# An output projection in seven half-size products per pair of token tiles, with every engine in program order up to a check

## The chip, the cores and the metric

The kernel runs on one core of a Trainium2 chip. The core has a matrix engine (TensorE, PE in the profile), a vector engine (VectorE, DVE), an activation engine (ScalarE, ACT), a general engine (GpSimd, POOL) and an engine that mostly issues transfers (SyncE, SP). Matrix products are written to PSUM[...]; the other data sit in SBUF, and large arrays in device memory, from and to which DMA transfers move them. The metric is the device time of one execution in microseconds (us); lower is better.

## The reference

An image of 48 by 48 tokens with 768 channels goes through a transformer block and then through a spectral layer. What matters here is the joint between attention and MLP:

```python
attn = softmax(q @ k^T * scale + rel_h + rel_w)      # 12 heads of 64
out  = attn @ v                                       # 2304 tokens x 768
out  = out @ proj_w + proj_b                          # <- the part that is changed
x    = shortcut + out
xn2  = layernorm(x)
h    = gelu(xn2 @ mlp_w1 + mlp_b1)
x    = x + (h @ mlp_w2 + mlp_b2)
# then the spectral layer: rfft2, two block-diagonal complex layers, irfft2, + x
```

All of it is in 32-bit floats. The output projection is a product of 2304 x 768 with 768 x 768.

## The kernel before, in words

The 2304 tokens are 18 tiles of 128 (`NT`), the 768 channels 6 blocks of 128 (`NC`); `CH` and `G` are 384[...]. The kernel runs in stages: queries, keys and values; attention for six pairs of heads, six chunks of 384 queries each; the output projection; the MLP in three passes of 768 tokens; the spectral layer.

**How the order is set.** A planner orders the instructions of each engine ahead of time by its own cost estimates. Inside a `tc.manual_schedule` region the engines it names keep the order in which the program writes them; where such a region's instructions fall among those of the same engine outside it remains the planner's. In attention PE, SP, ACT and DVE are in program order and POOL is the planner's. In the first half of the projection only PE is in program order. In the second half everything is the planner's.

**The end of attention.** For the last chunk, `left_apart` (L641) stores the inverse denominators, `spread_out` (L654) loads them back spread over the partitions, `scaled` multiplies (DVE, L666) and adds the value bias (POOL, L669), and `stored` (L675) writes the chunk to `oT` in device memory. Both transfers and the store are issued on SP.

**The projection.** `outputs(t)` (L754) loads one token tile `og` of `oT`, channels first. `residual(t)` loads a tile of the input into `x1` (L747) and adds the bias on POOL (L748). `projected(psum, t, og)` makes both 384-wide halves of the tile: six matmuls each into one bank (L761), then one DVE add of the bank into `x1` (L765). The weights `pw` are loaded during attention. `x1` lies in the buffer that holds the exponentials during attention, so a tile of `x1` can be loaded once the last chunk's products have read that part.

**The check and the two halves.** Attention skips the usual subtraction of the row maximum. The sums and the inverses of the denominators are therefore checked (L781 to L794), and a general path under `tc.If` (L801) recomputes attention where they are out of bounds; it is not taken with this data. Tiles 0 to 8 are projected before the check, tiles 9 to 17 after it. All engines meet at the check. In the second half the layer norm of tiles 0 to 5 (`normalise`, L121 to L129), their bias add (POOL, L995), the transposes to channels-first (`transposed`, L139 to L145) and the sums that the MLP's products need (`sums_of_tokens`, L177) are worked in between. The MLP's first weights and their sums on POOL (L159 to L168) are also moved up into it by the planner.

**Seven products instead of eight.** The queries, keys and values and the MLP already multiply blocked matrices by Strassen's scheme in Winograd's form: a 2 x 2 product of blocks takes seven block products and some sums of blocks instead of eight products. `left` and `right` make the sums of the two operands, and `queries_and_keys`, `values` and `hidden` (L1060) the products.

Of the kernel before, what the change touches and what calls it, by code (L numbers as in the profile page):

```python
# [22 lines left out]
NT = T // P  # L23
# [23 lines left out]
def block_then_afno(  # L47
# [69 lines left out]
    def normalise(pool, src, hat=None, made=None):  # L117

        stats = pool.tile([P, 2, 6], F32, name="stats")
        for i in range(2):  # L120
            nc.vector.bn_stats(stats[:, i, :], src[:, ts(i, C // 2)])  # L121
        mv = pool.tile([P, 2], F32, name="mv")
        nc.vector.bn_aggr(mv, stats.rearrange("p a b -> p (a b)"))
        rstd = pool.tile([P, 1], F32, name="rstd")
        nc.scalar.activation(rstd, mv[:, 1:2], AF.Sqrt, bias=eps)
        nc.vector.reciprocal(rstd, rstd)
        if hat is None:
            hat = pool.tile([P, C], F32, name="hat", bufs=4)
# [64 lines left out]
    with ExitStack() as flag_scope:  # L193
# [12 lines left out]
        with ExitStack() as att:  # L206
# [338 lines left out]
            with tc.manual_schedule(engines={mybir.EngineType.PE, mybir.EngineType.SP}):  # L545
# [123 lines left out]
                        nc.gpsimd.tensor_scalar(o, o, col(V_VB + pr), None, ALU.add)  # L669
                        results.append((pr, c, o))  # L670

                def stored():
                    while results:
                        pr, c, o = results.pop(0)
                        nc.sync.dma_start(out=oT[ts(pr, P), ts(c, G)], in_=o)  # L675

                def between(pr, c, acc):

# [28 lines left out]
                with tc.manual_schedule(  # L707
                    engines={mybir.EngineType.Activation, mybir.EngineType.DVE}
                ):
                    for pr in range(NC):  # L710
                        for c in range(T // G):
                            if c == 1 and pr < NC - 1:
                                fetch(pr + 1, kv[(pr + 1) % 2])
                            if c == 3 and pr < NC - 1:
                                fetch_values(pr + 1)
                            if c == 4 and pr == NC - 1:
                                nc.sync.dma_start(
                                    out=pw, in_=proj_w.rearrange("(c p) f -> p c f", p=P)
                                )
# [12 lines left out]
                            for i in range(6):  # L732
                                for what in work.get(i, ()):
                                    what()
                                products(op, heads[pr][2], range(3 * i, 3 * i + 3))
                            finish(pr, c, op)
                    scaled(0)
                    stored()

        ln2 = flag_scope.enter_context(tc.tile_pool(name="ln2", bufs=4))  # L740
        for i in range(4):
            ln2.tile([P, C], F32, name="hat")
        pj = flag_scope.enter_context(tc.tile_pool(name="proj", bufs=6))

        def residual(t):

            nc.sync.dma_start(out=x1[:, t, :], in_=x[ts(t, P), :])  # L747
            nc.gpsimd.tensor_tensor(x1[:, t, :], x1[:, t, :], pb, ALU.add)  # L748

        def outputs(t, og=None):  # L750

            if og is None:
                og = pj.tile([P, NC, P], F32, name="og")
            nc.sync.dma_start(out=og, in_=oT[:, ts(t, P)].rearrange("(c p) t -> p c t", p=P))  # L754
            return og

        def projected(psum, t, og):
            for k in range(2):
                pp = psum.tile([P, CH], F32, name="pp", tag="o")
                for c in range(NC):  # L760
                    nc.tensor.matmul(  # L761
                        pp, og[:, c, :], pw[:, c, ts(k, CH)], start=(c == 0), stop=(c == NC - 1)
                    )
                half = x1[:, t, ts(k, CH)]
                nc.vector.tensor_tensor(half, pp, half, ALU.add)  # L765

        EARLY = NT // 2
        with tc.tile_pool(name="ps_flag", bufs=1, space=PSUM) as psum, tc.tile_pool(  # L770
            name="ps_early", bufs=6, space=PSUM
        ) as psum_early, tc.manual_schedule(engines={mybir.EngineType.PE}):
            early = {t: outputs(t) for t in range(3)}
            pb = pj.tile([P, C], F32, name="pb", bufs=1)
            nc.sync.dma_start(out=pb, in_=proj_b[0, :].partition_broadcast(P))
            b2 = pj.tile([P, C], F32, name="b2_early", bufs=1)
            nc.sync.dma_start(out=b2, in_=mlp_b2[0, :].partition_broadcast(P))
            residual(0)
            projected(psum_early, 0, early[0])
# [7 lines left out]
            for t in range(1, EARLY):  # L787
                if t == 2:
                    line = psum.tile([1, P], F32, name="line")
                    nc.tensor.transpose(line, both, ident)  # L790
                    all_f = flag_pool.tile([1, 1], F32, name="all_f")
                    nc.vector.tensor_reduce(all_f, line, AX.X, ALU.min)
                    all_i = flag_pool.tile([1, 1], I32, name="all_i")
                    nc.vector.tensor_copy(all_i, all_f)  # L794
                residual(t)
                projected(psum_early, t, early[t] if t in early else outputs(t))
            for t in range(EARLY, NT):
                residual(t)
            later = {t: outputs(t) for t in range(EARLY, EARLY + 3)}
        safe = nc.values_load(all_i[0:1, 0:1], min_val=0, max_val=1)  # L800
        with tc.If(safe < 1):  # L801
            with ExitStack() as att:
# [27 lines left out]
                for pr in range(NC):  # L830
# [39 lines left out]
                    for sg in range(T // SG):  # L870
# [56 lines left out]
                        for j in range(2):  # L927
                            for qt in range(SG // P):
# [51 lines left out]
            with tc.tile_pool(name="g_ps_proj", bufs=2, space=PSUM) as psum:  # L980
                for t in range(NT):
                    residual(t)
                for t in range(EARLY):
                    projected(psum, t, outputs(t))
                for t, og in later.items():
                    outputs(t, og)

        with tc.tile_pool(name="ps_proj", bufs=2, space=PSUM) as psum:
            hats = []
            for t in range(EARLY, NT):  # L990
                projected(psum, t, later[t] if t in later else outputs(t))
                n = t - EARLY
                if n < 6:
                    hats.append(normalise(ln2, x1[:, n, :]))
                    nc.gpsimd.tensor_tensor(x1[:, n, :], x1[:, n, :], b2, ALU.add)  # L995
                if n in (2, 5):
                    transposed(psum, hats, xt, n // 3, V_LN2G, V_LN2B, tag="t")
                    hats = []
                if n == 5:
                    sums_of_tokens(xt, xs)  # L1000


    turn = ctx.enter_context(tc.tile_pool(name="turn", bufs=6))
# [585 lines left out]
```

## Time and profile before

| what | value |
|---|---|
| median of 3 runs | 2863.26 us (2861.73 to 2863.7) |
| the profiled execution | 2862.67 us, of which the span of the trace is 2860.6 us |
| PE busy | 2811.8 us, 98% of the span |
| DVE busy | 1695.7 us, 59% |
| ACT busy | 916.4 us, 32% |
| POOL busy | 625.5 us, 22% |
| first matmul of the projection | at 1429.92 us |
| last matmul of it before the check, first after it | ends near 1499.97, starts at 1503.69 us |
| first matmul of the MLP | at 1579.95 us |

Times of instructions are counted from the start of the span. One 32-bit matmul shows as two records, each with a weight load that runs beside it, so the 216 matmuls of the projection are 432 records. A busy PE is not a PE at its peak; the ends of matmuls are modelled.

### The profile page before, as it was taken

Reading aid. Unit: us, or ns where it says so; the run is one execution under the profiler, and the core shown is the slowest. Engines: PE = TensorE matmul, PEld = TensorE weight load, DVE = VectorE, ACT = ScalarE, POOL = GpSimd, SP = SyncE. Lnnn points to the kernel's source line nnn. Section 1 sums busy time; section 2 is a strip of 40 time slices with the busy share of each in tenths; the row PEclk is TensorE's granted clock in tenths of the full one; section 3 lists DMA queues with packets and bytes.
Section 4 is the critical chain, followed back from the end, with each engine's and each line's share of the span. In section 5 each row is a group of like instructions: output and inputs, shape, how many; then the busy total and the mean of one; then the engine's idle time right before and its main releaser. Section 6 shows DMA issues by size and latency. Waiting matters only on the chain. (4 is left out here: it accounts for less than half of the span.)

```text
span 2860.6 us, 41333 instructions
## 1 busy us (share of the span) xinstructions
PE 2811.8 (98%) x15877; PEld 1733.5 (61%) x15877; DVE 1695.7 (59%) x2488; ACT 916.4 (32%) x1466; POOL 625.5 (22%) x625
## 2 busy tenths in 40 slices
PE   8999999999999999999999999999999999999998
PEld 4555665656566666665555555555555555556887
DVE  5343226666666767676614666675666566666665
ACT  1011125757565666665400211021111211102332
POOL 2303010000000000000043332343232322222433
PEclk9999999999999999999999999999999999999999
DMA  4323285374663737455342121121121212113254
GB/s 154 129 97 111 97 164 108 64 131 76 94 134 57 132 65 128 93 80 99 107 133 78 50 67 55 56 86 59 54 67 55 89 55 66 45 62 113 61 160 141
DMA packets 223629, 262.80 MB, mean 92 GB/s; under 512 B 24668, under 2 KB 204092, under 8 KB 221888
## 3 DMA queue, kind: packets, MB, share of 16 engines
q1 hardware_dynamic: 220984, 258.22, 36.8%
q8 instruction: 129, 2.11, 0.3%
q10 hardware_dynamic: 2440, 1.84, 0.2%
q14 instruction: 76, 0.62, 0.1%
HBM read 143.96 MB, written 52.31 MB: 69 GB/s over the span
## 5 line engine op out<-in xcount | busy, mean ns | idle before, releaser
L581 ACT ACTIVATE main<-sp 128x768 f32<-128x768 f32 x648 | 516.4, 811 | 34.9 <-PE sp L571 19.9
L725 DVE TENSOR_TENSOR pairs<-pairs,main 128x1536 f32<-128x1536 f32 x252 | 443.1, 1758 | 27.1 <-DVE pairs L725 0.9
L571 PE MATMUL sp<-terms,select 64*128 64x384 f32 x1296 | 413.8, 631 | 0.0
L1122 DVE TENSOR_TENSOR main<-o,main 128x384 f32<-128x384 f32 x540 | 299.2, 557 | 39.4 <-PE o L1120 1.1
L1060 PE MATMUL h<-shared,w 128*128 128x384 f32 x864 | 296.6, 486 | 0.8 <-issue 0.8
L562 PE MATMUL sp<-shared 64*128 64x384 f32 x1296 | 266.9, 487 | 2.2 <-DVE o L462 2.2
L562 PE MATMUL sp<-qT,kT 64*128 64x384 f32 x1296 | 264.1, 484 | 0.0
L451 PE MATMUL m<-main 128*128 128x384 f32 x756 | 246.0, 487 | 3.3 <-DVE main L177 2.4
L1060 PEld LDWEIGHTS h<-shared,w 128*128 128x128 f32 x864 | 164.0, 190 | 116.2 <-issue 2.6
L1060 PE MATMUL h<-shared,w1s 128*128 128x384 f32 x648 | 226.6, 486 | 0.0
L627 POOL TENSOR_TENSOR inverse<-inverse,rden 24x32 f32<-24x32 f32 x36 | 15.1, 418 | 959.7 <-DVE sums L626 916.2
L594 PE MATMUL op<-main,shared 128*64 128x384 f32 x1296 | 217.4, 488 | 0.0
L1066 ACT ACTIVATE hT<-c,vec 128x384 f32<-128x384 f32 x108 | 66.3, 615 | 468.8 <-DVE c L1072 468.8
L594 PE MATMUL op<-main,v 128*64 128x384 f32 x1296 | 216.4, 488 | 0.0
L725 DVE TENSOR_TENSOR pairs<-main 128x1536 f32<-128x1536 f32 x36 | 63.3, 1759 | 250.6 <-ACT main L581 250.6
L451 PEld LDWEIGHTS m<-main 128*128 128x128 f32 x756 | 142.9, 190 | 103.8 <-issue 4.4
L1072 DVE TENSOR_TENSOR c<-h,u 128x384 f32<-128x384 f32 x108 | 60.2, 557 | 212.3 <-PE h L1060 212.3
L1120 PE MATMUL o<-w2s,hs 128*128 128x384 f32 x432 | 175.0, 487 | 4.0 <-DVE hs L160 4.0
L571 PEld LDWEIGHTS sp<-terms,select 64*128 64x128 f32 x1296 | 126.3, 187 | 83.5 <-issue 0.5
L1120 PE MATMUL o<-w,hT 128*128 128x384 f32 x432 | 175.0, 487 | 1.7 <-DVE acc L1126 0.8
L1060 PEld LDWEIGHTS h<-shared,w1s 128*128 128x128 f32 x648 | 123.2, 190 | 85.8
L159 POOL TENSOR_TENSOR w1s<-w 128x384 f32<-128x384 f32 x36 | 36.5, 1013 | 596.9 <-DMA w<-in_mlp_w_dram 396.9
(165 smaller groups left out, 3984.8 us busy)
## 6 DMA issues: line engine op xcount, KB each, us to landing
w<-in_mlp_w_dram SPq DMA_DIRECT2D x72, 768.0 KB
terms<-col_parts SPq DMA_DIRECT2D x432, 72.0 KB
terms<-row_hi SPq DMA_DIRECT2D x216, 72.0 KB
terms<-row_lo SPq DMA_DIRECT2D x216, 72.0 KB
main<-in_qkv_w_dram SPq DMA_DIRECT2D x36, 384.0 KB
z<-zt SPq DMA_DIRECT2D x48, 192.0 KB
x<-in_x_blocks_dram SPq DMA_DIRECT2D x18, 384.0 KB
k_d<-o SPq DMA_DIRECT2D x36, 192.0 KB
```

Of the source, the lines that this page charges most:

```text
L159: eng.tensor_tensor(s[0], a21, a22, ALU.add)
L451: nc.tensor.matmul(bank, a[:, c, :], b[:, c, :], start=(first and c == 0), stop=(c == 2), skip_group_check=not first,)
L562: nc.tensor.matmul(sp[:, j, :G], kT[at, ts(kt, P)], qT[at, ts(c, G)], start=first, stop=not first,)
L571: nc.tensor.matmul(sp[:, j, :G], select[at, a % 2], ready[pr, c][at, a // 2, b], start=first, stop=not first,)
L581: nc.scalar.activation(p, sp[:, :, :G], AF.Exp, scale=HD**-0.5)
L594: nc.tensor.matmul(op[ts(j, 64)], v[:, kt, ts(j, 64)], exps[:, kt, j, :], start=(kt == 0), stop=(kt == NT - 1),)
L725: nc.vector.tensor_tensor(pairs, so_far, exps[:, ds(kt - 1, 2)], ALU.add)
L1060: nc.tensor.matmul(bank[i], a[:, c, :], b[:, c, :], start=(start and c == 0), stop=(c == 2), skip_group_check=not start,)
L1066: nc.scalar.activation(h[:, i, ts(k, G)], src, AF.Gelu, bias=col(V_B1 + 2 * n + i))
L1072: nc.vector.tensor_tensor(t, src, other, ALU.add)
L1120: nc.tensor.matmul(bank[k], a, b, start=start, stop=True, skip_group_check=not start)
L1122: nc.vector.tensor_tensor(dst, bank[k], dst, ALU.add)
```

## The change

- The projection works on **pairs of token tiles**. `og` holds two tiles, and one transfer loads both.
- **The first pair is plain**: `plainly` makes four halves of six matmuls, each half in its own bank (m0 to m3), with a DVE add into `x1`.
- **Pairs 1 to 8** use seven half products: 3 channel blocks of `og` times a quarter of the weights, three matmuls for each of seven products (`projected`). The weight sums (`sum_of_weights`, four DVE operations of 128 x 1152) are made once; the fourth overwrites a quarter of `pw` after the first pair has read it. The sums of the outputs (`sums_of_outputs`, four DVE operations of 128 x 384) are made for each pair, one pair ahead.
- In each pair product 1 is copied to SBUF by ACT; DVE adds it to product 6 (`v`) and `v` to product 7 (`v7`); POOL adds `v`, `v` and `v7` into three of the four `x1` halves; DVE adds products 5, 2, 4 and 3 into `x1`. Products 2, 4 and 3 go to the banks of products 1, 7 and 5.
- **Four pairs** (eight tiles) come before the check and five (ten tiles) after it; before it was nine and nine.
- **Up to the check** PE, SP, DVE, ACT and POOL are all in program order; after it the planner orders all of them, as before.
- The **last store** of attention is issued on POOL instead of SP.
- In the second half the layer norms, the transposes and the sums for the MLP come after pairs instead of tiles.
- The general path reloads `pw`, projects plainly and makes the weight sums again; it is not taken.

```diff
-                def stored():
+                def stored(queue=nc.sync):
...
-                    stored()
+                    stored(nc.gpsimd)
...
-        pj = flag_scope.enter_context(tc.tile_pool(name="proj", bufs=6))
+        pj = flag_scope.enter_context(tc.tile_pool(name="proj", bufs=2))
+        pws = pj.tile([P, 3, 3, CH], F32, name="pws", bufs=1)
...
+        def weight_parts():
+            return [pw[:, ds(3 * j, 3), ts(k, CH)] for k in range(2) for j in range(2)]
+        def sum_of_weights(i):
+            a11, a12, a21, a22 = weight_parts()
+            s1, s2, s4 = (pws[:, i] for i in range(3))
+            dst, a, b, op = (
+                (s1, a21, a22, ALU.add), (s2, s1, a11, ALU.subtract),
+                (s4, a12, s2, ALU.subtract), (a21, a11, a21, ALU.subtract),
+            )[i]
+            nc.vector.tensor_tensor(dst, a, b, op)
+        def sums_of_outputs(pool, og):
+            b11, b21, b12, b22 = (og[:, ds(3 * i, 3), j] for j in range(2) for i in range(2))
+            sums = pool.tile([P, 3, 3, P], F32, name="ogs")
+            right(nc.vector, b11, b12, b21, b22, [sums[:, i] for i in range(3)])
+            return sums
...
+        def projected(psum, pool, u, og, sums):
...
+            pairs_of = {
+                1: (b11, a11), 2: (b21, a12), 3: (b22, s4), 4: (t4, a22),
+                5: (t1, s1), 6: (t2, s2), 7: (t3, s3),
+            }
+            bank = [psum.tile([P, G], F32, name=f"m{i}") for i in range(4)]
...
+            def first(j, k, src):
+                nc.gpsimd.tensor_tensor(half(j, k), half(j, k), src, ALU.add)
+            def into(j, k, src):
+                nc.vector.tensor_tensor(half(j, k), src, half(j, k), ALU.add)
+            m1 = pool.tile([P, G], F32, name="pm1")
+            nc.scalar.copy(m1, product(0, 1, True))
+            v = pool.tile([P, G], F32, name="pu")
+            nc.vector.tensor_tensor(v, product(1, 6, True), m1, ALU.add)
+            first(0, 1, v)
+            first(1, 0, v)
+            v7 = pool.tile([P, G], F32, name="pu7")
+            nc.vector.tensor_tensor(v7, product(2, 7, True), v, ALU.add)
+            first(1, 1, v7)
+            into(1, 1, product(3, 5, True))
+            into(0, 0, product(0, 2, False))
+            into(0, 1, product(2, 4, False))
+            into(1, 0, product(3, 3, False))
+        EARLY, PAIRS = 4, NT // 2
...
-        ) as psum_early, tc.manual_schedule(engines={mybir.EngineType.PE}):
-            early = {t: outputs(t) for t in range(3)}
+        ) as psum_early, tc.tile_pool(name="proj_early", bufs=2) as pe, tc.manual_schedule(
+            engines={
+                mybir.EngineType.PE, mybir.EngineType.SP, mybir.EngineType.DVE,
+                mybir.EngineType.Activation, mybir.EngineType.Pool,
+            }
+        ):
+            og = {0: outputs(0, pj)}
...
+            for i in range(2):
+                sum_of_weights(i)
+            for t in (2, 3):
                 residual(t)
...
+            plainly(
+                psum_early, 0, og[0],
+                ((partial(sum_of_weights, 2),), (partial(sums_ahead, 1),), (), ()),
+            )
+            sum_of_weights(3)
...
+            for u in range(1, EARLY):
+                if u < EARLY - 1:
+                    sums_ahead(u + 1)
+                else:
+                    kept[EARLY] = outputs(EARLY, pj)
+                    kept[EARLY + 1] = outputs(EARLY + 1, pj)
+                projected(psum_early, pe, u, og[u], ogs.pop(u))
+                for t in rest[: 5 if u < EARLY - 1 else NT]:
+                    residual(t)
...
-            for t in range(EARLY, NT):
-                projected(psum, t, later[t] if t in later else outputs(t))
+            for u in range(EARLY, PAIRS):
+                if u + 1 < PAIRS:
+                    if u + 1 not in kept:
+                        kept[u + 1] = outputs(u + 1, pl)
+                    ogs[u + 1] = sums_of_outputs(pl, kept[u + 1])
+                projected(psum, pl, u, kept[u], ogs.pop(u))
```

More of the change, by code (lines that the diff above doesn't have):

```diff
@@ L670, in scaled @@
                         results.append((pr, c, o))
-                def stored():
+                def stored(queue=nc.sync):
                     while results:
                         pr, c, o = results.pop(0)
-                        nc.sync.dma_start(out=oT[ts(pr, P), ts(c, G)], in_=o)
+                        queue.dma_start(out=oT[ts(pr, P), ts(c, G)], in_=o)
                 def between(pr, c, acc):
@@ L748, in residual, with outputs @@
             nc.gpsimd.tensor_tensor(x1[:, t, :], x1[:, t, :], pb, ALU.add)
-        def outputs(t, og=None):
+        def outputs(u, pool, og=None):
             if og is None:
-                og = pj.tile([P, NC, P], F32, name="og")
-            nc.sync.dma_start(out=og, in_=oT[:, ts(t, P)].rearrange("(c p) t -> p c t", p=P))
-            return og
[L757 to L760, printed above, removed]
+                og = pool.tile([P, NC, 2, P], F32, name="og", bufs=2)
+            nc.sync.dma_start(
+                out=og.rearrange("p c j t -> p c (j t)"),
+                in_=oT[:, ts(u, 2 * P)].rearrange("(c p) t -> p c t", p=P),
+            )
+            return og
@@ new lines, in sums_of_outputs, with plainly @@
+        def sums_of_outputs(pool, og):
[3 more added lines that the diff above has]
+            return sums
+        def plainly(psum, u, og, after=None):
+            for j in range(2):
+                for k in range(2):
+                    pp = psum.tile([P, CH], F32, name=f"m{2 * j + k}")
+                    for c in range(NC):
+                        nc.tensor.matmul(
+                            pp, og[:, c, j], pw[:, c, ts(k, CH)], start=(c == 0), stop=(c == NC - 1)
+                        )
+                    half = x1[:, 2 * u + j, ts(k, CH)]
+                    nc.vector.tensor_tensor(half, pp, half, ALU.add)
+                    if after:
+                        for what in after[2 * j + k]:
+                            what()
@@ new lines, in projected, with product @@
+        def projected(psum, pool, u, og, sums):
+            b11, b21, t3, b22 = (og[:, ds(3 * i, 3), j] for j in range(2) for i in range(2))
+            t1, t2, t4 = (sums[:, i] for i in range(3))
+            a11, a12, s3, a22 = weight_parts()
+            s1, s2, s4 = (pws[:, i] for i in range(3))
+            pairs_of = {
[3 more added lines that the diff above has]
+            bank = [psum.tile([P, G], F32, name=f"m{i}") for i in range(4)]
+            def product(i, k, first):
+                a, b = pairs_of[k]
+                for c in range(3):
@@ L761, in projected @@
                     nc.tensor.matmul(
-                        pp, og[:, c, :], pw[:, c, ts(k, CH)], start=(c == 0), stop=(c == NC - 1)
-                    )
-                half = x1[:, t, ts(k, CH)]
-                nc.vector.tensor_tensor(half, pp, half, ALU.add)
-        EARLY = NT // 2
-        with tc.tile_pool(name="ps_flag", bufs=1, space=PSUM) as psum, tc.tile_pool(
-            name="ps_early", bufs=6, space=PSUM
-        ) as psum_early, tc.manual_schedule(engines={mybir.EngineType.PE}):
-            early = {t: outputs(t) for t in range(3)}
+                        bank[i], a[:, c, :], b[:, c, :], start=(first and c == 0),
@@ new lines, in product, with half @@
+                        stop=(c == 2), skip_group_check=not first,
+                    )
+                return bank[i]
+            def half(j, k):
+                return x1[:, 2 * u + j, ts(k, CH)]
+            def first(j, k, src):
[4 more added lines that the diff above has]
+            nc.scalar.copy(m1, product(0, 1, True))
@@ new lines, in block_then_afno @@
+        EARLY, PAIRS = 4, NT // 2
+        kept = {}
+        with tc.tile_pool(name="ps_flag", bufs=1, space=PSUM) as psum, tc.tile_pool(
+            name="ps_early", bufs=1, space=PSUM
+        ) as psum_early, tc.tile_pool(name="proj_early", bufs=2) as pe, tc.manual_schedule(
[5 more added lines that the diff above has]
+            og = {0: outputs(0, pj)}
@@ L774, in block_then_afno @@
             pb = pj.tile([P, C], F32, name="pb", bufs=1)
             nc.sync.dma_start(out=pb, in_=proj_b[0, :].partition_broadcast(P))
+            residual(0)
+            og[1] = outputs(1, pj)
+            residual(1)
             b2 = pj.tile([P, C], F32, name="b2_early", bufs=1)
             nc.sync.dma_start(out=b2, in_=mlp_b2[0, :].partition_broadcast(P))
-            residual(0)
-            projected(psum_early, 0, early[0])
             total = flag_pool.tile([P, 2], F32, name="total")
@@ L786, in block_then_afno, with sums_ahead @@
             nc.vector.tensor_tensor(both, within[:, 0:1], within[:, 1:2], ALU.mult)
[L787 to L794, printed above, removed]
-                residual(t)
-                projected(psum_early, t, early[t] if t in early else outputs(t))
-            for t in range(EARLY, NT):
-                residual(t)
-            later = {t: outputs(t) for t in range(EARLY, EARLY + 3)}
+            for i in range(2):
+                sum_of_weights(i)
+            for t in (2, 3):
+                residual(t)
+            ogs = {}
+            def sums_ahead(u):
+                if u not in og:
+                    og[u] = outputs(u, pe)
+                ogs[u] = sums_of_outputs(pe, og[u])
+            plainly(
+                psum_early, 0, og[0],
+                ((partial(sum_of_weights, 2),), (partial(sums_ahead, 1),), (), ()),
+            )
+            sum_of_weights(3)
+            line = psum.tile([1, P], F32, name="line")
+            nc.tensor.transpose(line, both, ident)
+            all_f = flag_pool.tile([1, 1], F32, name="all_f")
+            nc.vector.tensor_reduce(all_f, line, AX.X, ALU.min)
+            all_i = flag_pool.tile([1, 1], I32, name="all_i")
+            nc.vector.tensor_copy(all_i, all_f)
+            rest = list(range(4, NT))
+            for u in range(1, EARLY):
[7 more added lines that the diff above has]
+                    residual(t)
+                    rest.remove(t)
         safe = nc.values_load(all_i[0:1, 0:1], min_val=0, max_val=1)
@@ L979, in block_then_afno @@
                                 )
-            with tc.tile_pool(name="g_ps_proj", bufs=2, space=PSUM) as psum:
+            with tc.tile_pool(name="g_ps_proj", bufs=2, space=PSUM) as psum, tc.tile_pool(
+                name="g_og", bufs=2
+            ) as gen_og:
                 for t in range(NT):
                     residual(t)
[L983 to L986, printed above, removed]
@@ L988, in block_then_afno @@
-        with tc.tile_pool(name="ps_proj", bufs=2, space=PSUM) as psum:
-            hats = []
-            for t in range(EARLY, NT):
-                projected(psum, t, later[t] if t in later else outputs(t))
[L992 to L999, printed above, removed]
+                nc.sync.dma_start(out=pw, in_=proj_w.rearrange("(c p) f -> p c f", p=P))
@@ new lines, in block_then_afno @@
+                for u in range(EARLY):
+                    plainly(psum, u, outputs(u, gen_og))
+                for u, og in kept.items():
+                    outputs(u, pj, og)
+                for i in range(4):
+                    sum_of_weights(i)
+        with tc.tile_pool(name="ps_proj", bufs=1, space=PSUM) as psum, tc.tile_pool(
+            name="ps_turn", bufs=2, space=PSUM
+        ) as psum_turn, tc.tile_pool(name="proj_late", bufs=2) as pl:
+            hats, ogs = [], {EARLY: sums_of_outputs(pl, kept[EARLY])}
+            for u in range(EARLY, PAIRS):
[4 more added lines that the diff above has]
+                projected(psum, pl, u, kept[u], ogs.pop(u))
+                n = u - EARLY
+                if n in (2, 3):
+                    transposed(
+                        psum_turn, hats[3 * (n - 2) :][:3], xt, n - 2, V_LN2G, V_LN2B, tag="t"
+                    )
+                if n == 3:
@@ L1000, in block_then_afno @@
                     sums_of_tokens(xt, xs)
+                if n < 3:
+                    for t in (2 * n, 2 * n + 1):
+                        hats.append(normalise(ln2, x1[:, t, :]))
+                        nc.gpsimd.tensor_tensor(x1[:, t, :], x1[:, t, :], b2, ALU.add)
     turn = ctx.enter_context(tc.tile_pool(name="turn", bufs=6))
```

## The prediction

> **What bounds the kernel now.** I read the page first: busy time of each engine.
>
> ```profile
> PE 2811.8 (98%) x15877; PEld 1733.5 (61%) x15877; DVE 1695.7 (59%) x2488; ACT 916.4 (32%) x1466; POOL 625.5 (22%) x625
> ```
>
> PE is busy for 98% of the span; a change pays where it removes matmuls and PE stays fed. So I asked for PE's instructions in order of time around the projection.
>
> ```profile
> 1425.28 4.06 PE L594 MATMUL op<-main,v 128*64 128x384 f32 x23
> 1429.92 15.75 PE L761 MATMUL pp<-col_parts,og 128*128 128x384 f32 x48 [0.58 <-ACT ot L635]
> 1445.51 0.27 PE L790 MATMUL line<-ident,both 128*1 128x128 f32 x1
> 1445.62 54.35 PE L761 MATMUL pp<-col_parts,og 128*128 128x384 f32 x168
> 1503.69 24.93 PE L761 MATMUL pp<-col_parts,og 128*128 128x384 f32 x72 [3.73 <-DVEq L801]
> ```
>
> From 1429.92 to 1503.69 us PE pauses only at the check, 3.73 us. The price of a matmul comes from the chain of work that ended last, where projection and MLP both appear:
>
> ```profile
> 1532.55 21.29 PE pp L761 x66
> 1614.00 5.80 PE h L1060 x18
> ```
>
> 21.29/66 and 5.80/18 are 0.3225 us a record. A matmul is two records: 0.645 us. The second row is three of the MLP's half products in a row, so half products cost PE no more per matmul. The 72 records after the check should take 23.2 us but took 24.93: 1.7 us lost. The windows show why:
>
> ```profile
> core 0: us, PE busy (x) PEld busy (x) DVE busy (x) ACT busy (x) POOL busy (x), PEclk, DMA share, GB/s
> 1429.90:1503.70 73.80, 70.05 (x218) 41.01 (x218) 12.03 (x22) 1.28 (x1) 33.06 (x20) 1.00 0.39 130
> 1503.70:1579.20 75.50, 75.45 (x252) 45.11 (x252) 34.24 (x70) 6.38 (x14) 27.42 (x22) 0.98 0.24 74
> ```
>
> The granted clock is 0.98 in the second half; 2% of 75.5 us is 1.5 us. DVE and POOL have more idle than busy time in both halves. The waits say that DVE waits for PE, not the reverse:
>
> ```profile
> DVE main L765 <- PE pp L761: 93.1, 31, 3.4
> POOL w1s L159 <- DMA w<-in_mlp_w_dram: 41.9, 2, 40.6
> ```
>
> Ledger of PE from 1429.92 to the MLP's first matmul at 1579.95: 216 x 0.645 = 139.3, transpose for the check 0.3, check 3.7, slow restart 1.7, 36 transposes at 0.11 (six take 0.66 in the chain) 4.0, the step to the MLP 0.8. Sum 149.8 against 150.0 measured; nothing else holds PE here.
>
> **What the Trainium skill says.** (1) "TensorE: Matmul & The Clock Gate", section "What's actually happening": after an idle window of about 3.4 us the PE runs at half clock until it has been busy as long. The trace agrees: 1.7 us lost behind a 3.73 us gap, none behind 0.58. (2) "GPSIMD Engine Reference", section 1: GpSimd shares its SBUF interfaces with VectorE, with contention where a DVE operation has two SBUF inputs. The trace agrees: the same DVE product of two SBUF tiles (L666) took 0.53 us at 1425.80 with POOL idle and 1.70 at 1433.55 beside POOL's adds, while adds with one input in PSUM (L765) stay at 0.54 to 0.56. (3) "DMA: Bandwidth & Descriptors", section "Specifications": first byte about 1 us from GpSimd's queue, 0.6 from SP's. The trace has no POOL transfer.
>
> **The change, part by part.** *Matmuls.* Pair 0 plain: 24. Eight pairs x 7 products x 3: 168. 192 instead of 216: -24 x 0.645 = **-15.5 us**. This is the whole gain.
>
> *Order on SP at the end of attention.* Before, SP issued og at 1417.52, ahead of attention's own last transfers:
>
> ```profile
> 1417.52 1.55 SPq L754 DMA_DIRECT2D og<-oT  x3
> 1425.85 0.32 SPq L641 DMA_DIRECT2D den_d<-rden  x1
> 1430.07 1.09 SPq L654 DMA_DIRECT2D spread<-den_d  x2
> ```
>
> The new region fixes SP's order within itself, but its place among attention's transfers stays the planner's, and og 0 is as ready as before. I take 0. If it comes behind them: denominators stored at 1425.85, a round trip of 1.3 us (1399.04 to 1400.32, the chunk before), spreads to 1428.2, store of the chunk before at 1428.3 behind its bias add, og 0 issued at 1428.9. Its 768 KB start 1.3 us later (data flow from about 1418.8 for the issue at 1417.52), need 2.2 us at the 350 GB/s seen here, plus some 0.7 us for the spreads in front and the completion: 1433.8 to 1434.5, **+4 to +5 us**. POOL's store is read by pairs 7 and 8 only, after the check; even 1 us of POOL hides.
>
> *DVE before the check.* Weight sums are 1152 elements; L177 has that shape, 3.90/3 = 1.3 us, four are 5.2. Sums of outputs: four of 384 at about 0.5 us, 2.0 a pair. Each pair has six adds from PSUM at 0.56, 3.4. So 5.4 us of the pair's 21 x 0.645 = 13.55: hidden. Tightest is pair 1: the plain pair ends at 1429.92 + 15.5 = 1445.4; then DVE's last plain add (0.6), the fourth weight sum (1.3), the check's reduce and cast (0.4) and the sums of pair 2 (2.0) precede `v`, which DVE reaches at 1449.7, when product 6 is due (1445.7 + 3.9 = 1449.6). At the contended rate (3.2 times) the two groups of sums take 7 us more and would cost PE 2 to 4. But x arrives for tiles 2 and 3 by about 1440 and POOL then rests. I take +0.5, 0 to 4.
>
> *SP and POOL before the check.* SP queues og, x and biases, 12 MB at 350 to 400 GB/s, 32 us of the 56; og 4 waits for pair 0's buffer and og 5 for pair 1's, tiles 14 to 17 of x behind it at about 1460: in time. POOL does 3 adds of 384 at 1.0 us (L159) and five residuals at 1.8 (L748: 19.44/11) in pairs 1 and 2: 12 of 13.55 us, hidden but narrow. Behind pair 3's adds (to 1480.3) come the last four residuals, 7.2 us, to 1487.5, while PE ends at 1445.7 + 3 x 13.55 = 1486.3. Before, DVE was last at 1500.5; all engines meet, so I take +0.5, 0 to 2. Gap and slow restart remain.
>
> *Within a pair.* With product 1 starting at 0: `v` at 3.87 + 0.56 = 4.4, `v7` at 5.8 + 0.56 = 6.4, POOL's three adds to 7.4, DVE adds product 5 at 7.7 to 8.3, and bank m3 is wanted by product 3 at 11.6: 3.3 us of slack; bank m2 (`v7` 6.4, product 4 at 9.7) has 3.3 as well, and the next pair's m0 (10.2, at 13.55) too. After the check DVE and POOL also normalise and sum MLP weights:
>
> ```profile
> 1515.15 0.55 DVE L765 TENSOR_TENSOR main<-pp,main 128x384 f32<-128x384 f32 x1
> 1519.49 0.54 DVE L765 TENSOR_TENSOR main<-pp,main 128x384 f32<-128x384 f32 x1
> 1508.69 1.00 POOL L159 TENSOR_TENSOR w1s<-w 128x384 f32<-128x384 f32 x1 [40.57 <-DMA w<-in_mlp_w_dram]
> ```
>
> Halves end at 1503.69 + 1.7 + n x 3.87: 1513.1 and 1517.0 for these adds, so DVE was 2.0 and 2.5 us late. POOL runs nearly solid from 1508.69 to 1537.5 in operations of 1.0 to 2.1 us. With `v` 2.0 late, one POOL operation of 2.1 in front and three adds at 1.2, product 5's add ends at 4.4 + 2.0 + 2.1 + 3.6 + 0.6 = 12.7 instead of 11.6: 1.1 us lost in pairs 4 and 5 each, none once that work is done. I take +2.2, 0 to 10. The LayerNorm work, transposes and token sums (5.2) still have the last pair's 13.55 us as cover; without it they would add up to 5.
>
> Sum: -15.5 + 0 + 0.5 + 0.5 + 2.2 = **-12.3 us**. 2862.67 (span 2860.6 and 2.07 around it) becomes 2850.4; that run lies 0.6 below the median 2863.26, so 2851.0 for the median.
>
> **The rivals.** *A, the sum above: 62%, 2847.3 to 2855.* For it: the PE ledger closes to 0.2 us, and every other engine has room.
>
> *B, og 0 comes late: 13%.* For it: SP is now written in program order; against: the region's place remains the planner's. 2851.0 + 4.5 = 2855.5.
>
> *C, the hand-over through POOL becomes the bound: 20%.* Place: `v` to POOL's three adds to product 5's add to bank m3. Price: each us beyond 3.3 of lateness stalls PE in that pair. In the five pairs after the check, where nothing orders POOL any more, 5 us late in each costs 5 x 1.7 = 8.5 (2857 to 2859). From 3.3 + 15.5/8 = 5.2 us late in all eight pairs the gain is gone; at 6 late, 8 x 2.7 = 22 lost, about 2869, slower than before. For it: POOL at 12 of 13.55 us before the check and solid after; against: its work after the check ends within two pairs. I give 8% to the part that still is faster, 6% to no change, 6% to slower.
>
> *D, the gain is given back in the MLP: 5%.* Now 3.2 of the first 25.8 us there have PE idle, behind DVE's normalising and ACT's table loads; more of that work pushed past the projection could eat 5 to 15 us: 2856 to 2866.
>
> **How the numbers follow.** A repeat of this kernel can tell about 0.2%, 5.7 us: faster is below 2857.5. A and B (75%), C's first part (8%) and some of D (1%) give 0.84, less 0.04 for planner effects elsewhere that I cannot name: 0.80 faster; same 0.10; slower 0.10. The range goes from the free case (-15.5, 2847.8, rounded down to 2847) to where B and the milder C end, 2860. Likeliest: 2851.0, its own range 2847.3 to 2855.
>
> **What would show it.** 384 matmul records instead of 432 in the projection, the MLP's first matmul near 1567.6, the check's gap near 4 us. Right: product 1 of pair 0 at about 1430. Wrong: PE waiting for DVE on product 3 or 4 (C), for og at the start (B), more than 3.2 us idle early in the MLP (D). A slow restart besides the check's would mean a stall over 3.4 us and cost another 1.7.

## The result, and the profile after

The changed kernel takes 2857.84 us (median of 20 runs, 2855.44 to 2860.64) against 2864.44 us (20 runs, 2861.73 to 2867.37): a ratio of 0.9978, with a 95% interval of 0.9971 to 0.9984. It is faster by 6.6 us, where the forecast had 12.3. The profiled execution has a span of 2856.1 us.

The busy times, from the page:

```profile
PE 2797.9 (98%) x15829; PEld 1724.1 (60%) x15829; DVE 1734.3 (61%) x2540; ACT 915.6 (32%) x1470; POOL 651.7 (23%) x650
```

PE is busy for 13.9 us less than before, and DVE has 52 operations more. So the matmuls did go; most of that time came back as time in which PE does nothing. PE's instructions in order of time (start, duration, line and operation; in brackets the idle time ahead and what ended it) show where:

```profile
1431.87 15.75 PE L786 MATMUL m<-col_parts,og 128*128 128x384 f32 x48 [0.58 <-ACT ot L635]
...
1492.35 2.82 PE L810 MATMUL m<-col_parts,og 128*128 128x384 f32 x6 [3.99 <-DVEq L898]
...
1546.83 2.20 PE L810 MATMUL m<-col_parts,ogs 128*128 128x384 f32 x6 [0.25 <-DVE pu L832]
...
1564.40 2.10 PE L810 MATMUL m<-pws,og 128*128 128x384 f32 x6
1576.24 3.58 PE L1170 MATMUL h<-shared,w 128*128 128x384 f32 x6 [9.74 <-DMA w<-in_mlp_w_dram]
```

From the projection's first matmul at 1431.87 to its last record at 1566.5 there is only the check (3.99 us, and a slow restart behind it) and one wait of 0.25. Then PE stands for 9.74 us before the MLP's first product. In the kernel before, that step took 0.8 us:

```profile
1579.95 2.17 PE L1060 MATMUL h<-shared,w 128*128 128x384 f32 x6 [0.80 <-issue]
```

The chain of work that ended last (start, duration, what) says what the 9.74 us consist of:

```profile
1566.60 0.35 SPq L1133
...
1567.62 8.10 DMA w<-in_mlp_w_dram
```

SP issues the MLP's bias (L1133, 384 KB) once the last pair's products are done, then a table of 768 KB, and only then the MLP's first weights, also 768 KB, whose landing takes 8.1 us. The waits of SP's queue agree: L1133 waited 31.2 us for PE's L810, the pairs' products. The bias and the table ahead of these weights, and further loads behind them, move in the same stretch; what they add to the 8.1 us was not tried. In the kernel before, SP issued the weights right after the check, 76 us ahead of their use:

```profile
1503.72 0.39 SPq L1037 DMA_DIRECT2D w<-in_mlp_w_dram  x1
```

The window of that gap (stretch and length, then busy time and instructions of PE, its weight loads, DVE, ACT and POOL; granted clock, share of the DMA engines, GB/s):

```profile
1566.40:1576.20 9.80, 0.10 (x1) 0.00 (x0) 9.52 (x25) 1.18 (x4) 4.47 (x3) 0.62 0.87 277
```

PE has one record in 9.8 us, while DMA is at 0.87 and DVE is busy throughout: it already normalises the next tokens.

Projection's first matmul to MLP's first, before and after: 150.03 and 144.37 us. The difference of -5.66 is made up of -15.48 for 24 matmuls at 0.645, +0.26 for the check's gap, +0.25 for the wait in a pair and +8.94 for the step to the MLP; +0.37 is left, some 0.2 of it in a slower restart behind the check. From the MLP's first matmul to the end it is 1280.65 and 1279.86 us, -0.8: in the MLP's first 26 us PE is busy for 25.11 us instead of 23.56, as would follow from DVE being ahead with its normalising, but the first records run slowly behind the gap. In all -6.45 us, close to the 6.6 of the medians. The two profiled executions themselves differ by 4.5 only, because this one reached the projection 1.95 us later. Single executions of one kernel differ by 1 to 3 us in these stretches (see the repeat below), so the small terms are not to be read finely.

### The profile page after: what moved, and what is told of

The parts are those of the page before. It is cut to its first block, busy times and chain, and to the rows that moved or that the text cites. A ratio compares the mean times of both kernels' runs of the same rounds, so it can differ in the third digit from the quotient of the medians.

```text
span 2856.1 us, 41310 instructions
## 1 busy us (share of the span) xinstructions
PE 2797.9 (98%) x15829; PEld 1724.1 (60%) x15829; DVE 1734.3 (61%) x2540; ACT 915.6 (32%) x1470; POOL 651.7 (23%) x650
## 5 line engine op out<-in xcount | busy, mean ns | idle before, releaser
L627 POOL TENSOR_TENSOR inverse<-inverse,rden 24x32 f32<-24x32 f32 x36 | 15.2, 422 | 929.1 <-DVE sums L626 887.5
L159 POOL TENSOR_TENSOR w1s<-w 128x384 f32<-128x384 f32 x36 | 36.9, 1024 | 547.0 <-DMA w<-in_mlp_w_dram 416.4
```

## The experiments

**The theory: the weights of the MLP come late because of where the pools lie in memory.** By the addresses of the built programs (no trace shows them; 1 KB is 1024 bytes), the projection's tiles end at 144 KB of each partition before the change and at 181 KB after it: the late pool `proj_late` now holds pairs of outputs, their sums and what `projected` keeps of its products, each twice. The MLP's first weights and their sums take 163 to 205 KB. Before, that room was free and they could load right after the check; by this theory they now can load only when the last pair has left it. The rivals: SP's queue or POOL's store at the end of attention (rival B's place), the hand-over through POOL (rival C), the order of the engines before the check.

### Free the weights' place

The late sums go to a pool at the other end of memory, and the late outputs into the early pool.

```diff
-        ) as psum_turn, tc.tile_pool(name="proj_late", bufs=2) as pl:
-            hats, ogs = [], {EARLY: sums_of_outputs(pl, kept[EARLY])}
+        ) as psum_turn, tc.tile_pool(name="proj_late", bufs=2) as pl, tc.tile_pool(
+            name="sums_late", bufs=2, side="right"
+        ) as sl:
+            hats, ogs = [], {EARLY: sums_of_outputs(sl, kept[EARLY])}
...
-                        kept[u + 1] = outputs(u + 1, pl)
-                    ogs[u + 1] = sums_of_outputs(pl, kept[u + 1])
+                        kept[u + 1] = outputs(u + 1, pj)
+                    ogs[u + 1] = sums_of_outputs(sl, kept[u + 1])
```

> The changed kernel with its late tiles moved out of the place of the MLP's weight buffers: the sums of outputs in a pool at the other end of SBUF, the late og tiles in the two buffers of the early ones. Nothing else. Theory M (the late pairs' tiles lie where the MLP's weight tiles go, so the weight loads wait for the last pair): the weight loads are issued within 2 us of the check instead of at 1567.6 us, the 9.7 us gap before the MLP's first matmul falls to about 1 us and its slow restart of about 2 us goes; 10 to 11 us less than the changed kernel, ratio to before 0.994 (0.993 to 0.995). Theory S (the loads are late because of how the pairs and their own loads are ordered, wherever the tiles lie): loads still late, ratio 0.998. Theory C of the prediction (once the weights are early, POOL's sums of them hold back POOL's adds into the halves): loads early, but PE waits for DVE at products 3 and 4, 3 to 10 us given back, ratio 0.995 to 0.998.

Measured: 2861.53 us, ratio 0.9992 (0.9986 to 0.9999), slower than any of the three cases foresaw. SP and PE in order of time:

```profile
1491.85 0.39 SPq L1149 DMA_DIRECT2D w<-in_mlp_w_dram  x1
```

```profile
1505.71 2.20 PE L810 MATMUL m<-pws,og 128*128 128x384 f32 x6 [2.00 <-DVE main L823]
1519.11 2.20 PE L810 MATMUL m<-col_parts,ogs 128*128 128x384 f32 x6 [1.51 <-DVE pu L832]
1528.35 4.21 PE L810 MATMUL m<-pws,og 128*128 128x384 f32 x6 [7.04 <-DVE main L823]
...
1579.50 2.17 PE L1172 MATMUL h<-shared,w 128*128 128x384 f32 x6 [0.80 <-issue]
```

The weights load right after the check again, and the step to the MLP is back at 0.80 us. So the pairs' tiles in that place were what held the weights back. But the gain does not appear: PE now waits 10.8 us among the pairs (these three and one of 0.25 later), and restarts slowly behind the 7.04. 9.0 of them are waits for a bank that DVE has not yet emptied; the other 1.8 are waits for `v7`, behind DVE's sums for the next pair, which take up to 1.35 us each beside POOL's work instead of 0.55. With the weights there, POOL has their sums to make as well. Ahead of the three adds of pair 5 it works almost without a pause from 1496.88 on; the end of that queue:

```profile
1523.06 1.80 POOL L1112 TENSOR_TENSOR main<-main,b_early 128x768 f32<-128x768 f32 x1
1524.81 2.89 POOL L820 TENSOR_TENSOR main<-main,pu 128x384 f32<-128x384 f32 x3
```

`v7` is ready at 1519.1; POOL comes to the adds at 1524.81 and DVE to product 5 at 1527.74:

```profile
1527.74 1.49 DVE L823 TENSOR_TENSOR main<-m,main 128x384 f32<-128x384 f32 x3 [8.69 <-POOL main L820]
```

DVE stands for 8.69 us, the banks stay full, and PE stops. This is rival C's path, in the two pairs in which the MLP's sums are made. Freeing the place saves 8.9 us and slow records at the MLP; the waits among the pairs take 10.8 and a slow restart, and the MLP's early idle time is back as well (PE busy for 23.11 of its first 26 us).

### Take the place away from the kernel before

A tile of 37.5 KB is laid where the pairs' tiles end in the changed kernel (144 to 181 KB) and held until the last projected tile. POOL gets a fill of 8 columns and one add of 8 columns more.

```diff
+        with tc.tile_pool(name="ps_proj", bufs=2, space=PSUM) as psum, tc.tile_pool(
+            name="over", bufs=1
+        ) as over:
+            held = over.tile([P, 9600], F32, name="held")
+            nc.gpsimd.memset(held[:, 0:8], 0.0)
...
+            nc.gpsimd.tensor_tensor(held[:, 0:8], held[:, 0:8], x1[:, NT - 1, C - 8 : C], ALU.add)
```

> The kernel before, with one more tile of 37.5 KB a partition over the place of the MLP's weight buffers, held until the last projected tile is done (two operations of 8 elements on POOL are added). Theory M: the weight loads move behind the projection and PE waits about 9 us there and restarts slowly; 10 to 11 us slower, ratio 1.0037 (1.002 to 1.005). Theory S: no change, ratio 1.000.

Measured: 2874.33 us, ratio 1.0038 (1.0024 to 1.0051), 10.8 us slower than the kernel before on the same chip (2863.54). The step to the MLP:

```profile
1591.95 4.18 PE L1065 MATMUL h<-shared,w 128*128 128x384 f32 x6 [9.32 <-POOL main L1181]
```

The bracket names a POOL add that ended just ahead of it, but SP issued the weights only after the last tile, 8.3 us before PE starts:

```profile
1583.64 0.43 SPq L1042 DMA_DIRECT2D w<-in_mlp_w_dram  x1
```

The kernel before, with nothing but that room taken, shows the changed kernel's gap: the place is enough to make it. The 10.8 us are not only this gap and the slow restart behind it, as had been expected. From the projection's first matmul to the MLP's it takes 160.78 us instead of 150.03: 8.5 are the gap, 1.3 a longer check (4.99 us instead of 3.73) and 1.0 slower records behind it; why the check took longer was not followed up. The slow records at the MLP (4.18 us instead of 2.17) are made up for later: from its first matmul to the end both kernels take some 1280.6 us.

### All pairs plain, the weights' place free

The version with the place free, with `plainly` in all nine pairs; no sums of weights or outputs are made.

```diff
-                projected(psum_early, pe, u, og[u], ogs.pop(u))
+                plainly(psum_early, u, og[u])
...
-                projected(psum, pl, u, kept[u], ogs.pop(u))
+                plainly(psum, u, kept[u])
```

> e1 with all nine pairs made plainly, in four halves of six matmuls, and no sums of weights or outputs: the same joint, 24 matmuls more. If a half product costs 3 x 0.645 us and nothing waits, this is 15.5 us more than e1, ratio to before about 0.9993 (0.998 to 1.0005). If the seven products lose time in their chain of adds (theory C), the difference to e1 is below 12 us.

Measured: 2866.23 us, ratio 1.0009 (1.0002 to 1.0015). That is just above the range that was foreseen, and only 4.7 us above the first experiment instead of 15.5: there the seven products lose most of what they save, as rival C has it. PE waits nowhere but at the check (3.75 us), and the MLP follows with 0.80. This is the new frame (pairs, the order of the engines, four pairs before the check) without the seven products: by itself it gains nothing. What the seven products are worth in that frame shows below against the version without waits.

### A repeat of the changed kernel

> The changed kernel as it is, beside the others on the same chip. Ratio 0.998. PE idle about 9.7 us before the MLP, weight loads issued after the last pair.

Measured: 2857.09 us, 0.9979 (0.9971 to 0.9987), with 9.54 us ahead of the MLP. Its profiled execution takes 145.24 us from the projection's first matmul to the MLP's and 1282.6 from there to the end, where the first one of this kernel took 144.37 and 1279.86.

### Let DVE write the banks out before POOL adds, in all pairs

POOL's three adds stand between `v7` and product 5's add on DVE, because both write the same halves of `x1`. Turned round, the bank is freed first and POOL adds later:

```diff
-            first(0, 1, v)
-            first(1, 0, v)
             v7 = pool.tile([P, G], F32, name="pu7")
             nc.vector.tensor_tensor(v7, product(2, 7, True), v, ALU.add)
-            first(1, 1, v7)
             into(1, 1, product(3, 5, True))
+            first(1, 1, v7)
             into(0, 0, product(0, 2, False))
             into(0, 1, product(2, 4, False))
+            first(0, 1, v)
             into(1, 0, product(3, 3, False))
+            first(1, 0, v)
```

With the weights' place free:

> e1 with one more edit: DVE adds each product into its x1 half first and POOL adds v or v7 to that half afterwards, so that no bank waits for POOL. Theory M+C (the late weights cost the changed kernel about 11 us, and in e1 early weights put POOL's weight sums ahead of POOL's adds, on which DVE and so the banks wait, about 13 us): both losses go; no PE wait over 1 us between the check and the MLP, MLP's first matmul about 134.5 us after the projection's first, ratio to before 0.995 (0.994 to 0.996). Theory D (e1 was slow because DVE itself is overloaded by what the early weights and hoisted LayerNorm bring): PE still waits for DVE in pairs 4 and 5, ratio 0.997 to 0.999.

In the changed kernel alone:

> The changed kernel with that order of adds alone, tiles as they were. Theory M+C: with late weights POOL has room, PE did not wait for the hand-over, so nothing is won: ratio 0.998 (0.997 to 0.9985), PE still waits 9 to 10 us before the MLP. Theory D or any cost of the hand-over in the changed kernel itself: 2 us or more faster.

Measured: 2856.92 us, 0.9976 (0.9968 to 0.9985), with the place free; 2863.36 us, 0.9998 (0.9990 to 1.0007), without, 6 us worse than the changed kernel and not foreseen by either case. The first ratio is the one foreseen for a DVE that has too much to do; the profile shows another cause. With the place free:

```profile
1491.92 4.18 PE L810 MATMUL m<-col_parts,og 128*128 128x384 f32 x6 [3.92 <-DVEq L898]
1497.96 3.67 PE L810 MATMUL m<-pws,ogs 128*128 128x384 f32 x6 [1.86 <-POOLq L898]
1522.26 2.20 PE L810 MATMUL m<-col_parts,ogs 128*128 128x384 f32 x6 [1.28 <-DVE pu L830]
```

The waits among the late pairs are gone but for these 1.28 us, and no bank is waited for any more: it was POOL's place in the hand-over. But POOL's last add before the check now starts at 1488.68 instead of ending at 1482.4, and its four last residuals follow:

```profile
1489.63 7.71 POOL L749 TENSOR_TENSOR main<-main,pb 128x768 f32<-128x768 f32 x4
```

They end at 1497.3, past the check, where in the changed kernel they end at 1489.5. Beside them DVE's first sums for the late pairs crawl: two take 3.69 us and the third 2.15, instead of 1.03 and 0.55, and PE's second product, which needs them, waits 1.86 us more and runs slowly again. (The bracket names POOL's queue, but DVE's third sum ends at 1497.75, just ahead of PE's 1497.96.) The MLP starts at 1571.81, with 0.80. So the turned order pays after the check and costs before it. In the changed kernel alone the same shows (two of DVE's sums take 3.21 us, the third 2.15, and PE's second product waits 2.42), and the 9.25 us ahead of the MLP stay. From the projection's first matmul to the MLP's it takes 148.25 us, 3.9 more than the changed kernel; what it loses beyond that comes later and was not followed up.

### The two together, each where it pays

The weights' place free, and the turned order in the five late pairs alone (`projected` gets an argument for it); the early pairs keep theirs.

```diff
+            if not banks_first:
+                first(0, 1, v)
+                first(1, 0, v)
...
-                projected(psum, pl, u, kept[u], ogs.pop(u))
+                projected(psum, pl, u, kept[u], ogs.pop(u), True)
```

> The late sums in memory of their own, so that the MLP's first weights load right after the check, and in the five late pairs alone DVE writes each half into its second place before POOL writes the first; the early pairs keep their order. If the late weights and the hand-over through POOL are the two things that cost the forecast its gain: the check's gap about 4 us as in the changed kernel, no wait of PE above 1.5 us in the late pairs, the MLP's first matmul 135 to 136 us after the projection's first one with at most 1 us of idle time before it, and a ratio of 0.9955 (0.9945 to 0.9965) to the kernel before. If DVE is too full in the late pairs (sums of weights, normalising and two writes per half), PE waits on DVE there and the ratio is 0.997 to 0.999.

And the turned late pairs with the weights late, as in the changed kernel:

> The changed kernel, its late sums where they were, with DVE writing each half into its second place before POOL writes the first in the five late pairs alone. Here the weights still load late, so POOL has no sums of weights among the pairs and this order has only 0.25 us of waits to save: if the order of the writes pays only where POOL is loaded, the ratio is 0.9975 to 0.9985, as the changed kernel, with 9 to 10 us of PE idle ahead of the MLP's first matmul. If the order of the writes brings the gain by itself, whatever the weights do: 0.996, as with both.

Measured: 2851.98 us, ratio 0.9959 (0.9945 to 0.9973), with both, from five runs of which the slowest (2854.01) is faster than any run of the changed kernel; 2857.24 us, 0.9979 (0.9969 to 0.9988), with the order alone. With both, SP issues the weights at 1492.01, and the step to the MLP is:

```profile
1567.43 2.17 PE L1180 MATMUL h<-shared,w 128*128 128x384 f32 x6 [0.80 <-issue]
```

The waits of PE in that stretch, complete:

```profile
PE m L810 <- DVEq L906: 3.9, 1, 3.9
PE h L1180 <- issue: 0.8, 1, 0.8
PE m L810 <- DVE pu L833: 0.7, 1, 0.7
PE m L786 <- ACT ot L635: 0.6, 1, 0.6
```

From the projection's first matmul (1431.59) to the MLP's it is 135.84 us, 14.2 less than before the change. The four versions side by side:

| | POOL adds first | DVE writes out first in late pairs |
|---|---|---|
| weights late | 0.9978 and 0.9979 | 0.9979 |
| weights right after the check | 0.9992 | **0.9959** |

Neither step pays alone; together they give the forecast's time, and the fastest version here. That they need each other is what the theory asks for: late weights keep their sums out of POOL's way, and early weights need a hand-over that doesn't pass through POOL. Against the version with all pairs plain (1.0009) the seven products are worth 0.0050, 14.3 us, of the 15.5 that PE's matmuls make.

### The last store, and the order of the engines

The last store of attention back on SP (`stored()`):

> The changed kernel with attention's last store issued on SP instead of POOL. By the changed kernel's trace the SP queue then waits for the bias add that ends at 1440.4, and og 2 and the loads of x behind it come up to 3 us later; they are wanted at 1449.8. All theories: no change against the changed kernel within 0.1%, ratio 0.998. If the joint hangs on SP's order there, PE waits at the start or in pair 1: 1 to 4 us slower.

Measured: 2857.82 us, 0.9979 (0.9971 to 0.9987): no effect. PE's step into the projection is 0.58 us with the store on either queue.

Then the engines that keep the program's order up to the check, taken back one after the other:

```diff
-            engines={
-                mybir.EngineType.PE, mybir.EngineType.SP, mybir.EngineType.DVE,
-                mybir.EngineType.Activation, mybir.EngineType.Pool,
-            }
+            engines={mybir.EngineType.PE}
```

PE alone:

> The changed kernel with only PE in program order before the check, as the kernel before had it; SP, DVE, ACT and POOL are the planner's there. The planner then puts the three weight sums on DVE ahead of attention's last denominators. If the fixed order matters: these 3 to 6 us of DVE come before the denominators and the inverse, which PE's last attention products do not wait for, but the check, spread and last scale do; 0 to 4 us slower, ratio 0.998 to 0.9995. If it doesn't: ratio 0.998. Weights of the MLP stay late in both cases.

PE and DVE:

> The changed kernel with only PE and DVE in program order up to the check; POOL, SP and ACT go where the planner puts them, and its order gives POOL ten residual adds in a row before its first adds of a half product. If it was DVE's order that made the kernel with PE alone in order 14 us slower than the changed one: 0.998 of the kernel before, as the changed kernel. If it was POOL's run of adds, beside which DVE's sums of two SBUF tiles crawl and behind which the first writes of a half come late: PE waits 5 to 10 us in pairs 1 and 2 and the ratio is 1.000 to 1.002.

PE and POOL:

> The changed kernel with only PE and POOL in program order up to the check; DVE, SP and ACT go where the planner puts them. If POOL's run of ten adds was what cost 14 us with PE alone, or PE and DVE, in order: POOL adds three times for each pair between its residuals as in the changed kernel, no operation of DVE above 4 us and no wait of PE above 1 us in pairs 1 to 3, and what stays is the 2.8 us that the denominators waited for DVE with PE alone in order: 0.998 to 0.9995 of the kernel before. If it was something else that DVE's, SP's or ACT's order brings: 1.002 again.

Measured: 2871.89 us, 1.0025 (1.0015 to 1.0034); 2871.48 us, 1.0023 (1.0015 to 1.0031); 2861.65 us, 0.9993 (0.9986 to 1.0). The first is far above what was expected. With PE and DVE in order, POOL, DVE and PE in order of time:

```profile
1441.36 17.64 POOL L749 TENSOR_TENSOR main<-main,pb 128x768 f32<-128x768 f32 x10
```

```profile
1441.15 18.27 DVE L167 TENSOR_TENSOR ogs<-og,ogs 128x384 f32<-128x384 f32 x1
```

```profile
1462.14 3.71 PE L810 MATMUL m<-col_parts,og 128*128 128x384 f32 x6 [10.95 <-DVE col_parts L772]
```

The planner lets POOL add ten residuals in a row as soon as x has arrived. Beside them one DVE sum of 0.56 us takes 18.27 us and ends as POOL's run does; the fourth weight sum comes behind it, and PE waits 10.95 us for it. In the changed kernel's order POOL first waits for pair 1's adds, at 1452.52, and the same sum takes 0.56. With POOL in order and DVE not, no such wait is left. What that version loses against the changed kernel is 2.78 us of PE at the end of attention, behind DVE's weight sums, and a slow restart there: the last records before the projection take 5.62 us instead of 4.06. So POOL's order up to the check is worth some 9 us with DVE out of order (1.0025 to 0.9993), and POOL's with SP's and ACT's some 13 with DVE in order (1.0023 to 0.9979). DVE's, with SP's and ACT's, is worth about 4 us beside an ordered POOL (0.9993 to 0.9979); DVE's alone is worth nothing without it (1.0025 to 1.0023).

## Why the prediction was right or wrong

- **The bound and the matmuls: right.** PE set the end, and 24 matmuls at 0.645 us went. Without waits the stretch is 14.2 us shorter.
- **Order on SP at the end of attention, 0: right.** The projection starts 0.58 us behind attention, as before; rival B didn't come.
- **DVE before the check, +0.5; SP and POOL before it, +0.5: near.** PE has no wait in pairs 1 to 3; the check and the restart behind it cost at most 0.6 more (0.26 and 0.37). "All engines meet" at the check is not how it went where POOL was late: in the version with the place free and the turned order in all pairs, PE goes on at 1491.92 while POOL's residuals from before the check run to 1497.3, and what that costs comes through DVE's sums. Also, the text took POOL's residuals to fall between the pairs without asking what that is worth. It is the program's order that sets it, and without it 9 to 13 us are lost. The 2 to 4 us that were set aside for two groups of contended sums were far too few for that case.
- **Within a pair, +2.2: inside its range by luck.** The step assumed the weights' sums on POOL right after the check, as before, and one POOL operation of 2.1 us ahead of the adds. In the changed kernel those sums have left the projection, and the step cost 0.25. Where they stay (the first experiment) pairs 4 and 5 lose 2.0 and 8.6 us instead of 1.1 each, and a slow restart: the path was named rightly, and sized for one operation where a whole queue stood ahead.
- **The step that failed: "the step to the MLP 0.8".** It stood in the ledger of the kernel before and was carried over without a word, and so was the early load of the weights. It measured 9.74 us, with slow records behind it. Those 8.94 us more would have left 3.4 of the 12.3; that it became 6.5 in the profiles is the cheap hand-over (0.25 instead of 2.2), a check 0.4 cheaper than allowed for, and 0.8 in the MLP. The change adds pools, and nobody had asked what then lies where the next stage's first loads go. "DVE and POOL have more idle than busy time" and "every other engine has room" look at engines; memory was the resource.
- **The rivals.** D, gain given back at the MLP with 5%, named the place but not the cause: its mark, over 3.2 us idle early in the MLP, isn't there, for once the MLP runs it idles less than before. C did not appear in the changed kernel and is what the freed version loses to.
- **The Trainium skill's pages held.** "TensorE: Matmul & The Clock Gate": behind 9.74 and 7.04 us of idle time the first records run slowly; behind gaps of 3.73 us, near the 3.4 it names, they did in some versions (4.18 us with PE and DVE in order) and not in others (2.17 with PE and POOL). "GPSIMD Engine Reference", section 1, on contention with DVE operations that have two SBUF inputs: DVE's sums of two SBUF tiles took from 2 to 33 times as long beside POOL's runs of adds; whether the contention alone makes the 33 was not shown. The 0.53 us that the prediction read at 1425.80 "with POOL idle" had POOL's L627 beside it from 1425.97 on; beside a POOL that was idle, the changed kernel's sum at 1441.57 took 0.56.

## What to carry to other kernels

When a change makes a stage's tiles larger, look at where they lie: here the next stage's first loads could be hidden only while no tile of the stage ahead occupied their place, and the busy times and waits of the profile before did not say that the change would take it. A hidden load also brings work with it: the version that hid it again lost more behind POOL than it won, until the hand-over left POOL out. And an order written out by hand may earn its time on an engine that is idle most of the span.

## What was not expected of the hardware

A DVE sum with both inputs in SBUF took 18.61 us with PE alone in order and 18.27 with PE and DVE, instead of 0.56, beside ten POOL adds without a pause (17.64 us); it ended as they did. Beside the runs of four or five residuals in the other versions such sums took 1.1 to 2.2 us and got through while POOL was still at work. What shuts DVE out for the whole run in one place and only slows it in the other was not tried.
